# Row sums of a small-attention group: from GpSimd additions in SBUF to identity matmuls on TensorE in PSUM

## Chip, cores and metric

One NeuronCore of a Trainium2 chip runs the whole kernel in a single launch. The metric is the device time of one execution in microseconds. The kernel before took 4007.05 us, the median of three runs (4005.77 to 4012.08).

## What is computed

The input x is [8, 512, 256] in fp32, and four residual layers follow each other, each on a layer norm of x:

```python
x = x + attn_a(layernorm(x))   # 16 heads of C = 64; see below
x = x + ffn(layernorm(x))      # silu gate, two gelu layers of 1024, back to 256
x = x + attn_b(layernorm(x))   # ordinary causal attention over 512 tokens, 16 heads of 16
x = x + ffn(layernorm(x))      # the same weights again
```

Attention A is the odd one. It attends not over tokens but over the 64 channels of one head of one token:

```python
Q, K, V = (x @ W + b).reshape(b, s, 16, 64)       # Q scaled by 1/8
scores[q, k] = Q[q] * K[k]     for k <= q          # an outer product per head and token
w = softmax(scores, axis=k)
attn[q] = sum_k w[q, k] * V[k]
x_out = attn.reshape(b, s, 1024) @ Wo + bo
```

So nothing of the scores is a matmul: each token and head has a 64x64 triangle of products, exponentials and weighted sums, with tokens on the partitions.

## The kernel before

**Groups and units.** Attention A goes through 8 batches b, 4 groups of heads g (4 heads, GW = 256 channels) and 4 token tiles i of 128: 128 groups. In each group the triangle is cut into a diagonal and squares: squares of 32 rows and columns, then of 16, 8, 4, 2 and 1. They make four units u: unit 0 is the squares of 32 of heads 0 and 1, unit 1 the squares of 16 of all four heads, unit 2 the squares of 32 of heads 2 and 3, unit 3 all smaller squares. Units 0 to 2 have 2048 scores per token and use a work tile w of 4096 elements, which holds the exponentials in one half and the exponentials times V in the other; unit 3 has 1920 and uses the tile ws.

**One unit's way.** `scores` (the multiplication at L784) writes Q times K: for units 0 and 2 on GpSimd, for units 1 and 3 on VectorE, which reads Q from the PSUM tile qv. `exps` (L798) takes the exponential on ScalarE. `weigh` (L808) multiplies by V on VectorE, again with qv in PSUM as one operand. `halve` (L814), for units 0 to 2, is a DMA issued from GpSimd's queue that adds one half of the columns of w onto the other, 1 MB each. `fold` (L819), for units 0 and 2, halves once more on GpSimd. `gather` (L845) reduces what is left along the columns to row sums red, on VectorE. The diagonal's exponential and its product with V are in acc, [128, 2, 256]: plane 0 for the denominators, plane 1 for the numerators.

**Ending a group.** `add_rows` (L852) adds the row sums of each size to the rows of acc to which they belong, on GpSimd, seven additions per group; for squares of 2 and 1 `small_squares` takes them from ws itself, after an addition of pairs (L835). `invert` (L856) is VectorE's reciprocal of plane 0, `divide` (L860) GpSimd's product. `turn_group` (L868) transposes plane 1 on TensorE, ScalarE copies it to att (L719), `project_out` (L876 and L472) multiplies by Wo and adds x, and `new_x` (L887) copies the new x back.

**Buffers.** The PSUM tile `bank` is one bank of two halves of 256 columns. `half_bank` hands the halves out in turn, to the layer norm's transpose, the projection of K (`project`, L741), `turn_group` and `project_out`. qv, the projection of Q and V (L746), has two buffers. Tile w has three buffers for units 0 and 2; unit 1 has a tile of its own, w16, with one; ws has one.

**What sets the order.** The order of TensorE, VectorE, ScalarE and GpSimd is the order of the program text (`manual_schedule`). Each engine works off its own queue in order. Step n of `AttentionA.step` begins unit n and does the later work of earlier units: `self.at(n - 2)` is the unit that began two steps ago. So a group is four steps, and "n - 5 with u == NU - 1" means five steps after the group's last unit began. Each step has three parts, parted by `yield`. After each part the main loop takes as many pieces from the second stream (FFN, attention B, FFN of the batch that A has finished) as a planned cost allows: `total = 309.5` units per batch, spread evenly over its 64 steps, beginning after the first 64 steps and eleven more. That stream is `after_a`; its ffn matmuls are L1052, L1120 and L1146. In the first batch attention A is alone, after the last one the stream is alone.

The scheduling of the group's end before, cut from the step:

```python
b, i, g, u = self.at(n - 5)
if u == NU - 1:
    self.invert(b, i, g)
...
yield
...
for args in self.sums:
    self.add_rows(*args)
...
```

Of the kernel before, what the change touches and what calls it, by code (L numbers as in the profile page):

```python
# [284 lines left out]
def fast_path(ctx: ExitStack, tc: tile.TileContext, k, t, flag):  # L285
# [196 lines left out]

    bank = ps_a.tile([P, 2, GW], F32, name="bank")
    halves = [0]

    def half_bank():
        halves[0] ^= 1
        return bank[:, halves[0], :]
# [115 lines left out]
    class AttentionA:  # L604
# [3 lines left out]
        def __init__(self):  # L608
            self.x = {0: x_first}
            self.rn, self.live = {}, {}  # L610
            self.w = {(0, 0): fitted[0]}
            self.wo = {}
            self.load_wo(0, 0)
            self.ready, self.sums = set(), []
            self.todo = [
                (b, i, g, u) for b in range(NB) for g in range(NG) for i in range(NT) for u in range(NU)
            ]
            self.steps = len(self.todo) + 11
# [19 lines left out]
        def step(self, n):  # L638

            weighed = self.at(n - 2)  # L640
            if weighed[0] is not None:
                self.weigh(*weighed)
            unit = self.at(n)
            on_pool = unit[3] in (0, 2)
            if on_pool:
                half = self.scores(*unit)
                next(half)
            if weighed[0] is not None:
                self.halve(*weighed)
            if on_pool:  # L650
# [11 lines left out]
            if u == NU - 1:  # L662
                self.invert(b, i, g)
            b, i, g, u = self.at(n - 4)
            if u == 1:
                self.gather(b, i, g, u)
            b, i, g, u = self.at(n + 7)
            if u == 0 and g == 0:
                nc.scalar.copy(self.live[b, i], self.live.pop("ps_ln"))
            if self.at(n - 1)[0] is not None:  # L670
                self.exps(*self.at(n - 1))
            yield
            if unit[0] is not None and not on_pool:
                for _ in self.scores(*unit):
                    pass
            for args in self.sums:
                self.add_rows(*args)
            self.sums = []
            b, i, g, u = self.at(n - 5)
            if u == NU - 1:  # L680
                self.divide(b, i, g)
            b, i, g, u = self.at(n - 2)
            if u == NU - 1:
                self.small_squares(b, i, g)

            b, i, g, u = self.at(n - 4)
            if u == 0:
                self.fold(b, i, g, u)
# [3 lines left out]
            b, i, g, u = self.at(n - 9)  # L692
            if u == NU - 1:
                self.new_x(b, i, g)
            b, i, g, u = self.at(n + 2)
            if u == 0:
                self.keep_qk(b, i, g)
            b, i, g, u = self.at(n - 7)
            if u == NU - 1:
                self.turn_group(b, i, g)  # L700
            b, i, g, u = self.at(n - 8)
# [9 lines left out]
            b, i, g, u = self.at(n - 5)  # L711
            if u == 0:
                self.gather(b, i, g, u)
# [3 lines left out]
            b, i, g, u = self.at(n - 7)  # L717
# [3 lines left out]
            if u == 0 and g == 0:  # L721
                self.live[b, i] = lnp.tile([P, DC, P], F32, tag="xnt_a", name=f"xnta_{b}_{i}", bufs=NT)
                self.live["ps_ln"] = turned_over(self.live.pop("xn"), half_bank().rearrange("p (c s) -> p c s", c=DC))
# [11 lines left out]
        def project(self, b, i, g):  # L735
# [3 lines left out]
            pk = half_bank()  # L739
# [25 lines left out]
        def scores(self, b, i, g, n_u):  # L765
# [6 lines left out]

            if n_u in (0, 2):
                w = wt.tile([P, 4096], F32, tag="w", name=f"w_{b}_{i}_{g}_{n_u}", bufs=3)
            elif n_u == 1:
                w = wt.tile([P, 4096], F32, tag="w16", name=f"w16_{b}_{i}_{g}")
# [3 lines left out]
            eng, q = (nc.gpsimd, kt[:, 1]) if n_u in (0, 2) else (nc.vector, qv[:, 0])  # L780
# [47 lines left out]
        def small_squares(self, b, i, g):  # L828

            w = self.live[b, i, g, NU - 1]  # L830
            for n, off, nsq, cols in squares(units[NU - 1]):
                if n <= 2:
                    both = self.columns_of(w, n, off, nsq)
                    if n == 2:
                        nc.gpsimd.tensor_tensor(both[..., :1], both[..., :1], both[..., 1:], ALU.add)  # L835
                    self.add_rows(b, i, g, n, cols, both[..., 0])

        def gather(self, b, i, g, n_u):


            w = self.live.pop((b, i, g, n_u))
            for n, off, nsq, cols in squares(units[n_u]):
                if n > 2:
                    red = ap_.tile([P, 2, nsq * n], F32, tag=f"red{nsq * n}", name=f"red_{b}_{i}_{g}_{n_u}_{n}", bufs=2 + (n < 32))
                    nc.vector.tensor_reduce(red, self.columns_of(w, n, off, nsq), AX.X, ALU.add)  # L845
                    self.sums.append((b, i, g, n, cols, red))

        def add_rows(self, b, i, g, n, cols, part):

            acc = self.live[b, i, g][2]  # L850
            rows = acc[:, :, cols].rearrange("p a (x t) -> p a x t", t=2 * n)[..., n:]
            nc.gpsimd.tensor_tensor(rows, rows, part.rearrange("p a (x i) -> p a x i", i=n), ALU.add)  # L852

        def invert(self, b, i, g):
            acc = self.live[b, i, g][2]
            nc.vector.reciprocal(acc[:, 0, :], acc[:, 0, :])  # L856

        def divide(self, b, i, g):
            acc = self.live[b, i, g][2]
            nc.gpsimd.tensor_tensor(acc[:, 1, :], acc[:, 1, :], acc[:, 0, :], ALU.mult)  # L860

        def turn_group(self, b, i, g):
# [3 lines left out]
            pt = half_bank().rearrange("p (c s) -> p c s", c=nch)  # L866
# [577 lines left out]
```

## Time and profile before

| What | Value |
|---|---|
| median of three runs | 4007.05 us |
| the profiled execution | 4009.55 us |
| its span | 4007.6 us |
| PE busy | 2958.0 us, 74% |
| DVE busy | 3376.7 us, 84% |
| ACT busy | 2337.2 us, 58% |
| POOL busy | 3098.1 us, 77% |
| DMA, mean rate | 167 GB/s |

The engines are PE (TensorE matmuls), PEld (its weight loads, which overlap the matmuls), DVE (VectorE), ACT (ScalarE), POOL (GpSimd) and SP (SyncE, which here issues DMAs). A line such as L784 is a line of the kernel before. A group of instructions is shown as line, engine, operation, output <- inputs by the program's names, shapes, count, then busy us in total, mean ns of one, and the engine's idle time just ahead of them with what ended it. A window row has its start and end, its length, the busy us of PE, PEld, DVE, ACT and POOL (with the number of instructions), the granted TensorE clock as a share of full speed, the mean busy share of the 16 DMA engines and their GB/s. In the records each fp32 matmul of the program appears twice.

### The profile page before, as it was taken

The page shows a single profiled execution, that of the slowest core. Times are in us where ns is not written, and L with a number is a line of the kernel's source. Part 1 is how long each engine was busy: PE and PEld are TensorE (multiplying, and loading weights), DVE is VectorE, ACT ScalarE, POOL GpSimd, SP SyncE. Part 2 cuts the span into 40 slices and gives each one's busy share as a digit, 9 for nine tenths or more (in the row PEclk, how much of TensorE's full clock was granted, in tenths as well). Part 3 has the DMA queues.
Part 4 walks back from the last instruction along what each step waited for, and adds up shares of the span by engine and source line. Part 5 has one row for each costly group of instructions (what it writes and reads, how often), then busy time and mean ns, then how long its engine had stood idle before and what let it go on. Part 6 is the DMA issues. An engine that isn't in the chain of part 4 may idle for free.

```text
span 4007.6 us, 37678 instructions
## 1 busy us (share of the span) xinstructions
PE 2958.0 (74%) x12328; PEld 2012.2 (50%) x12328; DVE 3376.7 (84%) x3777; ACT 2337.2 (58%) x3145; POOL 3098.1 (77%) x3051
## 2 busy tenths in 40 slices
PE   1543478777876888768787788768787778768988
PEld 0311145355653656346553566346653556436847
DVE  4899988998889888998989988998889988897115
ACT  2433465666755766666755767567656667555342
POOL 6688888887888887887888888888888878886211
PEclk7555689888987989889897889879898899879999
DMA  8566777668776777668776688668877687767304
GB/s 240 114 141 145 146 182 182 147 161 199 199 162 126 195 188 196 150 147 210 174 192 139 168 198 214 147 131 198 195 181 151 154 199 205 155 133 210 126 29 167
DMA packets 118653, 671.07 MB, mean 167 GB/s; under 512 B 12704, under 2 KB 31915, under 8 KB 43824
## 3 DMA queue, kind: packets, MB, share of 16 engines
q0 software_dynamic: 78336, 570.46, 62.9%
q1 hardware_dynamic: 40112, 98.11, 6.8%
q8 instruction: 100, 1.64, 0.2%
q14 instruction: 105, 0.86, 0.1%
HBM read 255.90 MB, written 9.96 MB: 66 GB/s over the span
## 4 chain that ended last, share of the span: by engine, by line
DVE 38%; PE 16%; POOL 14%; DMA 12%; issue 8%; ACT 8%; POOLq 0%; DVEq 0%; ACTq 0%
DVE red L845 15%; DMA w<-w 12%; DVE w L808 10%; PE ph L1120 5%; ACT w L798 3%; POOL w L819 3%; DVE ws L808 3%; POOL w L784 3%; PE pqkb L1167 3%; DVE ws L784 3%; POOL acc L852 3%; DVE w L784 2%; POOL w L814 2%; DVE acc L856 2%; POOL h L1036 2%
## 5 line engine op out<-in xcount | busy, mean ns | idle before, releaser
L798 ACT ACTIVATE w<-w 128x2048 f32<-128x2048 f32 x384 | 734.2, 1913 | 653.8 <-POOL w L784 440.8
L1120 PE MATMUL ph<-h,hidden 128*128 128x512 f32 x4096 | 1047.9, 412 | 77.4 <-POOL h L1036 45.5
L784 POOL TENSOR_TENSOR w<-k 128x1024 f32<-128x1024 f32 x512 | 1076.2, 2102 | 9.6 <-ACT k L762 9.0
L1120 PEld LDWEIGHTS ph<-h,hidden 128*128 128x128 f32 x4096 | 795.3, 196 | 282.1 <-POOL h L1036 55.9
L808 DVE TENSOR_TENSOR w<-w,qv 128x1024 f32<-128x1024 f32 x768 | 899.8, 1213 | 22.4 <-ACT w L798 22.3
L845 DVE TENSOR_REDUCE red<-w 128x128 f32<-128x1024 f32 (+1 forms) x384 | 601.8, 1567 | 171.6 <-DMA w<-w 94.6
L819 POOL TENSOR_TENSOR w<-w 128x1024 f32<-128x1024 f32 x256 | 643.1, 2512 | 72.5 <-DMA w<-w 71.9
L814 POOL DMA_DIRECT2D w<-w x384 | 337.1, 878 | 339.7 <-issue 134.8
L852 POOL TENSOR_TENSOR acc<-acc,red 128x256 f32<-128x256 f32 (+1 forms) x640 | 471.0, 736 | 152.3 <-DVE red L845 124.5
L845 DVE TENSOR_REDUCE red<-ws 128x256 f32<-128x2048 f32 (+1 forms) x256 | 435.5, 1743 | 0.0
L746 PE MATMUL qv<-wqv,xnta 128*128 128x512 f32 x512 | 299.3, 715 | 89.9 <-DVE ws L808 82.4
L808 DVE TENSOR_TENSOR ws<-ws,qv 128x1024 f32<-128x1024 f32 (+3 forms) x512 | 294.7, 638 | 49.4 <-ACT ws L798 49.4
L1052 PE MATMUL pw<-xnt,gate 128*128 128x512 f32 (+2 forms) x1152 | 298.8, 419 | 24.9 <-ACT silu L1028 18.0
L784 DVE TENSOR_TENSOR w<-qv,k 128x1024 f32<-128x1024 f32 x256 | 301.3, 1219 | 3.6
L784 DVE TENSOR_TENSOR ws<-qv,k 128x1024 f32<-128x1024 f32 (+3 forms) x512 | 299.8, 648 | 0.0
L868 PE MATMUL bank<-ident,acc 128*128 128x128 f32 x256 | 64.3, 341 | 287.5 <-ACT k L761 287.1
L798 ACT ACTIVATE ws<-ws 128x1920 f32<-128x1920 f32 x128 | 231.5, 1809 | 75.3 <-DVE ws L784 74.7
L1052 PEld LDWEIGHTS pw<-xnt,gate 128*128 128x128 f32 x1152 | 227.6, 213 | 82.1 <-ACT silu L1028 22.3
L1229 ACT ACTIVATE eb<-psb 128x256 f32<-128x256 f32 (+3 forms) x512 | 182.2, 443 | 146.6 <-PE psb L1226 146.3
L1146 PE MATMUL pof<-w,h 128*128 128x256 f32 x1024 | 247.9, 396 | 19.4 <-ACT h L1085 19.4
L1085 ACT ACTIVATE h<-ph,s_sb 128x512 fp32r<-128x512 f32 (+1 forms) x256 | 171.1, 688 | 145.9 <-PE ph L1120 144.6
L856 DVE RECIPROCAL acc<-acc 128x256 f32<-128x256 f32 x128 | 223.2, 1744 | 12.3 <-POOL acc L852 12.3
(143 smaller groups left out, 4723.5 us busy)
## 6 DMA issues: line engine op xcount, KB each, us to landing
w<-w POOLq DMA_DIRECT2D x384, 1024.0 KB, 7.7
hidden<-in_h POOLq DMA_DIRECT2D x128, 1024.0 KB, 7.9
gate<-in_w12p POOLq DMA_DIRECT2D x32, 1024.0 KB, 9.0
w<-w_d SPq DMA_DIRECT2D x16, 1024.0 KB, 12.0
wqv<-wqv_d SPq DMA_DIRECT2D x31, 512.0 KB
wo<-in_wo SPq DMA_DIRECT2D x32, 256.0 KB, 7.4
wbqk<-wbqk_d SPq DMA_DIRECT2D x8, 1024.0 KB
w<-in_h SPq DMA_DIRECT2D x8, 1024.0 KB, 7.0
```

The source lines that it names most:

```text
L746: nc.tensor.matmul(qv.rearrange("p j f -> p (j f)"), xnt[:, c, :], wqv[:, c, :], start=(c == 0), stop=(c == DC - 1),)
L784: eng.tensor_tensor(e, rows(q).to_broadcast(shape), columns(kt[:, 0]).to_broadcast(shape), ALU.mult)
L798: nc.scalar.activation(e, e, AF.Exp, scale=C**-0.5)
L808: nc.vector.tensor_tensor(ev, e, columns(qv[:, 1]).to_broadcast(list(e.shape)), ALU.mult)
L814: nc.gpsimd.dma_start(w[:, :2048], w[:, 2048:], accum_op=ALU.add)
L819: nc.gpsimd.tensor_tensor(w[:, :1024], w[:, :1024], w[:, 1024:2048], ALU.add)
L845: nc.vector.tensor_reduce(red, self.columns_of(w, n, off, nsq), AX.X, ALU.add)
L852: nc.gpsimd.tensor_tensor(rows, rows, part.rearrange("p a (x i) -> p a x i", i=n), ALU.add)
L856: nc.vector.reciprocal(acc[:, 0, :], acc[:, 0, :])
L1052: nc.tensor.matmul(pj[:, toks], w[:, m % 4, j, c, :], xs[:, p, c, toks], start=(p == 0 and c == 0), stop=(p == 1 and c == DC - 1),)
L1120: nc.tensor.matmul(pss[j], w[:, j, c, :], h_in(p, c), start=(p == 0 and c == 0), stop=(p == 1 and c == MC - 1),)
L1146: nc.tensor.matmul(po, h(0, c)[:, i * P : (i + 1) * P], w3[:, c, :], start=(c == 0), stop=False)
```

## The change

Five things change together.

1. `add_up` replaces `add_rows` and `small_squares`. On TensorE, the identity as the stationary operand, a first matmul copies acc (512 columns) into `bank`, and eight more add the row sums to the strided rows of it to which they belong: the sums of the squares of 32 (two, 128 columns each), of 16, 8 and 4 (256 each) from red, those of 2 as two matmuls of 256 columns (one for each column of the square) and those of 1 (256) straight from ws. Both halves of `bank` are taken while this lasts.
2. `divide` takes reciprocal and product on VectorE, with `bank` as an operand of both; the result is written to acc as before.
3. The scores of unit 1 (the squares of 16) go to GpSimd: two pieces of 1024 elements per partition.
4. Units 0, 1 and 2 share one rotation of four w tiles; w16 is gone. The red tiles have one buffer for each unit and size.
5. The halves of `bank` are fixed: half 0 for layer norm and K, half 1 for turn and output. The steps are placed anew (below); unit 0's halve is put ahead of both score pieces of unit 2; the lag at which the second stream starts falls from eleven steps to ten; and in `after_a` the first batch's four tiles of layer norm are set off with a flush and 0.8 units of cost each.

The steps after the group's last unit, before and after (part in brackets): row sums 1 to 4 by size -> `add_up` 4 [2]; reciprocal 5 [1] and product 5 [2] -> both 5 [1]; turn 7 [2] -> 6 [1]; output product 8 [2] -> 7 [2]; new x 9 [2] -> 8 [1].

The core of the diff:

```diff
             unit = self.at(n)
-            on_pool = unit[3] in (0, 2)
-            if on_pool:
+            large = unit[3] in (0, 1, 2)
+            if weighed[0] is not None and weighed[3] == 0:
+                self.halve(*weighed)
+            if large:
                 half = self.scores(*unit)
                 next(half)
-            if weighed[0] is not None:
+            if weighed[0] is not None and weighed[3] > 0:
                 self.halve(*weighed)
...
+            b, i, g, u = self.at(n - 4)
+            if u in (0, 1):
+                self.gather(b, i, g, u)
...
             b, i, g, u = self.at(n - 5)
             if u == NU - 1:
-                self.invert(b, i, g)
+                self.divide(b, i, g)
...
+            b, i, g, u = self.at(n - 6)
+            if u == NU - 1:
+                self.turn_group(b, i, g)
             yield
...
+            b, i, g, u = self.at(n - 4)
             if u == NU - 1:
+                self.add_up(b, i, g)
...
             b, i, g, u = self.at(n - 3)
             if u == NU - 1:
                 self.gather(b, i, g, u)
+            if u == 0:
+                self.fold(b, i, g, u)
+            if unit[0] is not None and not large:
+                for _ in self.scores(*unit):
+                    pass
...
-            if n_u in (0, 2):
-                w = wt.tile([P, 4096], F32, tag="w", name=f"w_{b}_{i}_{g}_{n_u}", bufs=3)
-            elif n_u == 1:
-                w = wt.tile([P, 4096], F32, tag="w16", name=f"w16_{b}_{i}_{g}")
+            if n_u < NU - 1:
+                w = wt.tile([P, 4096], F32, tag="w", name=f"w_{b}_{i}_{g}_{n_u}", bufs=4)
             else:
                 w = wt.tile([P, 2 * SMALL], F32, tag="ws", name=f"ws_{b}_{i}_{g}")
-            eng, q = (nc.gpsimd, kt[:, 1]) if n_u in (0, 2) else (nc.vector, qv[:, 0])
+            eng, q = (nc.gpsimd, kt[:, 1]) if n_u < NU - 1 else (nc.vector, qv[:, 0])
...
+        def add_up(self, b, i, g):
             acc = self.live[b, i, g][2]
+            parts = self.live.pop(("parts", b, i, g))
+            nc.tensor.matmul(bank, ident, acc, start=True, stop=False)
+            for j, (n, cols, part) in enumerate(parts):
+                rows = bank[:, :, cols].rearrange("p a (x t) -> p a x t", t=2 * n)[..., n:]
+                part = part.rearrange("p a (x i) -> p a x i", i=n)
+                nc.tensor.matmul(rows, ident, part, start=False, stop=j == len(parts) - 1)
 
         def divide(self, b, i, g):
             acc = self.live[b, i, g][2]
-            nc.gpsimd.tensor_tensor(acc[:, 1, :], acc[:, 1, :], acc[:, 0, :], ALU.mult)
+            nc.vector.reciprocal(acc[:, 0, :], bank[:, 0])
+            nc.vector.tensor_tensor(acc[:, 1, :], bank[:, 1], acc[:, 0, :], ALU.mult)
...
         for i in range(NT):
             head(0, i)
+            flush()
+            yield 0.8
...
-                while 3 * spent * each < total * (3 * (n - each - 11) + part + 1):
+                while 3 * spent * each < total * (3 * (n - each - 10) + part + 1):
```

## The prediction, made before the result

> **What bounds the kernel now.** I read the page's engine totals first, then its chain of what ended last.
>
> ```profile
> span 4007.6 us, 37678 instructions
> PE 2958.0 (74%) x12328; PEld 2012.2 (50%) x12328; DVE 3376.7 (84%) x3777; ACT 2337.2 (58%) x3145; POOL 3098.1 (77%) x3051
> DVE 38%; PE 16%; POOL 14%; DMA 12%; issue 8%; ACT 8%; POOLq 0%; DVEq 0%; ACTq 0%
> ```
>
> VectorE is fullest, GpSimd second, TensorE close behind. The totals mix stages, so next the windows by stage (columns: window, length, then busy us of PE, PEld, DVE, ACT, POOL, then granted clock, DMA share, GB/s).
>
> ```profile
> 86.00:473.00 387.00, 160.76 (x347) 84.94 (x347) 357.53 (x373) 145.71 (x147) 312.05 (x274) 0.56 0.66 140
> 473.00:1394.00 921.00, 700.54 (x2920) 472.42 (x2920) 832.03 (x937) 579.31 (x777) 769.02 (x757) 0.86 0.73 171
> 1394.00:1634.00 240.00, 195.36 (x754) 143.53 (x754) 205.89 (x229) 153.34 (x187) 195.53 (x198) 0.90 0.78 190
> 1634.00:1855.00 221.00, 164.87 (x774) 102.96 (x774) 208.55 (x240) 145.29 (x214) 187.95 (x181) 0.85 0.70 159
> 1855.00:3588.00 1733.00, 1351.03 (x5772) 922.75 (x5772) 1559.53 (x1744) 1114.91 (x1499) 1442.20 (x1411) 0.87 0.74 175
> ```
>
> The 128 reciprocals (L856), one per group, are the clock of attention A. In the first stage (A alone) they follow each other by 23.7 us and VectorE never rests. From 473 us on, with the feed-forward stream (FFN and attention B) beside A, they average 28.70 us (475.6 to 3574.8 us, 108 steps); there VectorE is busy 832+206+209+1560 = 2806 of 3115 us, 25.9 per group, and TensorE 2412 us, 22.2 per group. So A alone is bound by VectorE; the mixed stage has 2.8 us of VectorE idle per group and 6.5 us of TensorE idle. After 3588 us A runs out and the last stream is alone; the change doesn't touch that tail. The prices come from groups by shape, window 500 to 3500 us (104 groups), then the lone-A stage.
>
> ```profile
> L784 POOL TENSOR_TENSOR w<-k 128x1024 f32<-128x1024 f32 x416 | 875.5, 2105 | 0.6
> L784 DVE TENSOR_TENSOR w<-qv,k 128x1024 f32<-128x1024 f32 x208 | 244.8, 1219 | 2.8
> L852 POOL TENSOR_TENSOR acc<-acc,red 128x256 f32<-128x256 f32 x311 | 236.4, 760 | 114.9 <-DVE red L845 92.2 <-PE pyt L1268 5.7
> L852 POOL TENSOR_TENSOR acc<-acc,ws 128x256 f32<-128x256 f32 x208 | 166.0, 798 | 16.3
> L852 POOL TENSOR_TENSOR acc<-acc,red 128x128 f32<-128x128 f32 x208 | 145.4, 699 | 0.0
> L860 POOL TENSOR_TENSOR acc<-acc 128x256 f32<-128x256 f32 x104 | 106.3, 1022 | 0.0
> L835 POOL TENSOR_TENSOR ws<-ws 128x256 f32<-128x256 f32 x104 | 72.8, 700 | 0.0
> L856 DVE RECIPROCAL acc<-acc 128x256 f32<-128x256 f32 x104 | 181.4, 1744 | 11.1 <-POOL acc L852 11.1
> ...
> L746 PE MATMUL qv<-wqv,xnta 128*128 128x512 f32 x48 | 45.0, 1094 | 23.0 <-DVE ws L808 17.4 <-issue 5.7
> ```
>
> The timeline near 2015 us gives what runs of matmuls really occupy (start, length).
>
> ```profile
> 2014.85 1.02 PE L741 MATMUL bank<-wk,xnta 128*128 128x256 f32 x4
> 2015.71 1.88 PE L746 MATMUL qv<-wqv,xnta 128*128 128x512 f32 x4
> ...
> 2024.38 0.41 PE L868 MATMUL bank<-ident,acc 128*128 128x128 f32 x2 [1.33 <-ACT k L761]
> ```
>
> **What the skill says.** "FP8 and Floating Point Precision", TensorE Precision Notes: true fp32 takes four passes. The trace shows two records per fp32 matmul, and L746's four records (two matmuls of 512 columns) have weight loads 0.43 us apart, so 1.72 us, 1.68 ns a column. "TensorE: Matmul & The Clock Gate", What's actually happening: an idle array runs at half clock. The trace agrees: lone-A clock 0.56, L746 at 1094 ns. "GPSIMD Engine Reference", Engine selection: GpSimd has no way to PSUM, so with sums there the quotient must go elsewhere; no row shows GpSimd on PSUM.
>
> **The change, part by part, per group.**
> GpSimd loses seven additions (L852: 3x0.76 + 2x0.80 + 2x0.70 = 5.3), the product (1.02) and the pair sum (0.70): -7.0 us. It gains two score pieces, 2x2.1 = +4.2. Net -2.8. GpSimd isn't on the loop below, so this gains nothing by itself; it gives back some of the DMA slack lost below.
> VectorE loses two pieces, 2x1.22 = -2.4. It gains the quotient's product; the nearest PSUM-reading row of that size (L771) takes 0.42. The reciprocal now reads PSUM: 1.74 taken; at least that, since no reason makes it shorter, at most 0.1 more. Net -2.0: 25.9 becomes 23.9.
> TensorE gains nine identity matmuls over 512 + 128 + 256 + 128 + 256 + 256 + 2x256 + 256 columns (acc, the squares of 32, 16, 32, 8, 4, 2 as two, 1): 2304 columns x 1.68 = 3.9, plus weight loads on the short ones; I take 4.2. Matmuls with strided reads and writes have no row: 3.9 if the stride is free, since columns can't cost less than contiguous ones, and 7.8 at half clock (4.2 x 1094/592, the full-clock length of L746). Total 22.2 + 4.2 = 26.4, now above VectorE.
> Steps: the first fold, turn, output product and new x come one step earlier. What each issues goes along: the wo load on SP's queue moves up with the output product, with a group's length before its data are used; keep_qk moves up within its step on ACT, which is busy 19 of 28.7 us. Cost nil under that cover; without it, one copy, 0.4 us per group. The stream and so the tail begin one of four steps sooner: -28.7/4 = -7 us once. The stagger at the stream's head (four flushes) lies beside A; uncovered it would be a few us once.
> Halves: the first w's DMA had 20.7 us of VectorE work between weighing and its reduction (two reductions of ws and one of w 4.6, three weighings 7.0, L784 for ws and w16 4.7, L845 of w16 2.3, L771 and L856 2.2), now 11.6 (4.6, two weighings 4.6, ws scores 2.4); less the 2.5 us fold, 9.1 stay. The squares of 16 get 10.8 for 9.1, the third w 8.6 for 10.5. DMA landing is 7.8 us in median, 16.7 at most, in the mixed stage. Zero in lone A (8.0 at most), up to a few us where weights load. With the rotation of four, scores on GpSimd wait for a reduction at least one step old: nil.
>
> **The new wait** is what decides. ws has one buffer and the row sums read it on TensorE. So VectorE's small scores must wait until the last identity matmul ends, and behind them on VectorE stand the third weighing, the first reduction and the quotient; TensorE's turn waits for the quotient, and the whole stream stands behind the turn. That is a closed loop, whose length no slack shortens:
> on VectorE, small scores to quotient: 2.26 + 2.26 + 1.13 + 0.34 + 1.66 + 0.35 = 8.0 (scores, third weighing, first reduction, L771, reciprocal, product, as the timeline's starts follow each other), plus 5/12 of the stream's 2.2 us (L1031, L1091, L524, L983, L525, L1262 over 104 groups) = 8.9;
> on TensorE, turn 0.4, projection 0.86 + 1.72 = 2.6, output 1.3, seven of twelve parts of the stream (22.2 less A's own 4.3 = 17.9, so 10.4), row sums 4.2: 18.9.
> Sum 27.8; a hand-over is short (the att copy starts 0.03 us after the turn's end at 2024.8). TensorE's idle today is 6.5 per group, 2.2 of it at the turn (226.4 us over 104 groups), which the loop replaces; of the other 4.3, seven twelfths, 2.5, can lie in the loop. Bounds: 0 to 2.5; I take 1.4: less than the bound, since TensorE no longer runs ahead of ACT, but late DMAs are in it. Result 29.2: +0.5 over 28.7, x112 groups = +56 us.
> Lone A: 8.0, then VectorE's 11.5 from the quotient to the last reduction (weighings 2.2 and 2.6, reductions 2.2, 1.1 and 3.3), then the four matmuls that need it or come after, eight passes: 4.2 us at half clock (L876 there: 52 records in 26.9 us), 1.7 at full. So 23.7 or 21.8 (VectorE's own 23.7 - 1.9) against 23.7: bounds 0 and -1.9. I take -0.4, the clock being low in this stage: x15 = -6 us.
> Sum: 56 - 6 - 7 = +43. The profiled execution took 4009.55 us, so 4052.6; the median of the runs is 2.5 less: 4050.
>
> **The rivals.**
> A: faster. The half-clock share of TensorE's time vanishes as it gets denser, and the idle inside the loop is near 0. Then dense groups (half, PE 195 of 240 us) stay as they are, light ones gain 0.6: -34; lone A gains all 1.9: -28; -7. 3940. For it: clock 0.85 to 0.90 now, and both fullest engines get lighter. Against: the loop. It decides where the mean reciprocal distance falls under 28.82 (28.70 + 13/112).
> B: worse. The idle in the loop is the full 2.5 and DMAs past 9.1 us stop the first reduction inside it: +1.4 x 112 - 13 = +144: 4150. For it: in the dense stretch (1394 to 1634 us) VectorE already waited 12.8 us for the w DMA and 11.6 for the fold behind it, in 8 groups.
> C: gain and loss cancel: the mixed stage at +0.1, near 4005.
>
> **Chances.** Forecast 0.47, A 0.30, B 0.10, C 0.13. Under 0.2% this kernel's measurement tells nothing, so C splits 0.04 faster, 0.09 same. Faster 0.34, same 0.09, slower 0.57. Range 3920 to 4170: it takes in A's and B's centres with about 0.1 left out below and 0.06 above; the forecast alone is 4000 to 4100.
>
> **What would show it.** Right: VectorE idle before the small scores with TensorE as releaser, some us per group; reciprocals about 29 us apart; PE near 26 us per group; lone A near 23.3. Wrong: that wait absent or under 1 us with reciprocals below 28.5 apart (the loop isn't the bound), row sums far from 4.2 us, or VectorE's added idle ending on DMA w instead.

## The result and the profile after

The changed kernel takes 4330.07 us (median of four runs) against 4009.57 us for the kernel before on the same chip: 1.0801 times as long, 95% interval 1.0783 to 1.0820. The forecast was 4050 us with a range up to 4170: the direction came out as forecast, the size is outside the range. The profiled execution has a span of 4328.0 us, 320.4 more than before.

In the listings of the changed kernel the lines are numbered anew: scores are L769, exps L783, weigh L793, halve L799, fold L804, the reductions L821, the copy of acc into the bank L830, the other row sums L834, reciprocal and product L838 and L839, the turn L847, the output product L855 and L472, the new x L866, the projections of K and of Q and V L729 and L734, the copy of K out of the bank L749, the turn of the stream's layer norm L544.

First the page's span, engine totals and chain of the changed kernel.

```profile
span 4328.0 us, 41431 instructions
...
PE 3405.4 (79%) x14632; PEld 2385.9 (55%) x14632; DVE 3154.8 (73%) x3649; ACT 2360.3 (55%) x3161; POOL 2851.6 (66%) x2155
...
PE 43%; DVE 26%; ACT 12%; POOL 9%; issue 7%; DMA 3%; SPq 0%; ACTq 0%; POOLq 0%; DVEq 0%
```

VectorE and GpSimd did get lighter (by 222 and 246 us), and TensorE took 447 us more. No engine is above 79%, yet the kernel is 8% longer. The chain of what ended last has changed hands: TensorE 43% (16% before), VectorE 26% (38%). Next the windows of the changed kernel for A alone and for the mixed stage, then that of the kernel before for the same mixed stretch.

```profile
86.00:473.00 387.00, 209.26 (x640) 127.47 (x639) 348.29 (x380) 157.89 (x158) 304.52 (x181) 0.74 0.71 150
```

```profile
600.00:3600.00 3000.00, 2454.88 (x10722) 1733.04 (x10721) 2272.00 (x2653) 1770.18 (x2361) 2077.90 (x1565) 0.91 0.67 158
```

```profile
600.00:3600.00 3000.00, 2332.86 (x9957) 1588.78 (x9958) 2704.22 (x3034) 1921.17 (x2591) 2495.06 (x2452) 0.87 0.74 173
```

The second row is the changed kernel, the third the one before. In the mixed stage every engine but TensorE does less in the same 3000 us, and the DMAs move 158 instead of 173 GB/s: the whole kernel waits for something. A group's reciprocals are 31.84 us apart there (from the 17th to the third last), 28.81 before; in A alone (2nd to 15th) 22.30 against 23.88. The account of the 320.4 us: up to the 17th reciprocal the changed kernel is 13.4 us ahead (485.9 against 499.3 us, although its first reciprocal comes 13.7 us later, at 100.0 instead of 86.3); from there to the last reciprocal it loses 332.6 us (3521.7 against 3189.1); behind that the tail is as long as before (320.4 and 319.2). So all of the loss lies in the mixed stage.

The waits of the changed kernel say for what, in 600 to 3700 us (columns: engine, what it wanted and its line, the releaser; us in total, times, longest).

```profile
DVE ws L769 <- PE bank L834: 521.6, 90, 11.0
POOL w L799 <- DVE w L793: 518.9, 154, 9.6
ACT ws L783 <- DVE ws L769: 221.9, 44, 8.6
...
PE bank L847 <- DVE acc L839: 136.5, 46, 6.1
```

The first line is the wait that the prediction named: VectorE stands before the small scores until the last identity matmul has read ws, 5.3 us for each of the 98 groups whose small scores start in this window. The second and third are what stands behind it: GpSimd's halve and ScalarE's exponentials wait for VectorE in turn. In A alone the same wait is 1.3 us once, in 200 to 500 us.

One round of the loop, in the timeline of TensorE and then of VectorE (start, length):

```profile
2010.74 0.59 PE L472 MATMUL pof<-x,ident 128*128 128x256 f32 x2
2011.17 0.38 PE L847 MATMUL bank<-ident,acc 128*128 128x128 f32 x2
...
2024.15 0.69 PE L544 MATMUL ps_ln<-ident,xn 128*128 128x128 f32 x2 [4.21 <-ACT xn L534]
...
2027.67 1.92 PE L830 MATMUL bank<-acc,ident 128*128 128x512 f32 x2
2029.38 3.62 PE L834 MATMUL bank<-red,ident 128*128 128x128 f32 x10
2032.79 1.73 PE L834 MATMUL bank<-ws,ident 128*128 128x256 f32 x6
2034.17 5.84 PE L1031 MATMUL pw<-xnt,gate 128*128 128x512 f32 x24
```

```profile
2007.49 0.42 DVE L839 TENSOR_TENSOR acc<-bank,acc 128x256 f32<-128x256 f32 x1
...
2018.18 3.40 DVE L821 TENSOR_REDUCE red<-ws 128x256 f32<-128x2048 f32 x2
...
2034.56 2.35 DVE L769 TENSOR_TENSOR ws<-qv,k 128x1024 f32<-128x1024 f32 x4 [4.31 <-PE bank L834]
...
2042.33 0.42 DVE L839 TENSOR_TENSOR acc<-bank,acc 128x256 f32<-128x256 f32 x1
```

VectorE ends the quotient at 2007.91. TensorE turns it only at 2011.17, behind stream matmuls that stood earlier in its queue. Then come A's projection, stream, output product, and a stretch in which TensorE waits for the layer norm of a stream tile (4.21 us before L544). The row sums begin at 2027.67 although the last reduction they read had ended at 2021.6. They read ws last, so VectorE starts the next small scores at 2034.56, and the next quotient ends at 2042.75: one round of 34.8 us.

### The profile page after: what moved, and what is told of

Its sections match the earlier page's. It is cut to its first block, busy times and chain, and to the rows that moved or that the text cites. A ratio compares the mean times of both kernels' runs of the same rounds, so it can differ in the third digit from the quotient of the medians.

```text
span 4328.0 us, 41431 instructions
## 1 busy us (share of the span) xinstructions
PE 3405.4 (79%) x14632; PEld 2385.9 (55%) x14632; DVE 3154.8 (73%) x3649; ACT 2360.3 (55%) x3161; POOL 2851.6 (66%) x2155
## 4 chain that ended last, share of the span: by engine, by line
PE 43%; DVE 26%; ACT 12%; POOL 9%; issue 7%; DMA 3%; SPq 0%; ACTq 0%; POOLq 0%; DVEq 0%
PE ph L1099 12%; PE bank L834 8%; DVE w L793 7%; DVE red L821 7%; POOL w L769 4%; DVE acc L838 3%; PE qv L734 3%; DVE ws L769 3%; ACT w L783 3%; PE bank L830 3%; PE pqkb L1146 3%; PE pw L1031 2%; DMA w<-w 2%; PE bank L855 2%; PE pyb L1213 2%
## 5 line engine op out<-in xcount | busy, mean ns | idle before, releaser
L769 POOL TENSOR_TENSOR w<-k 128x1024 f32<-128x1024 f32 x768 | 1601.4, 2240 | 9.3 <-ACT k L750 9.3
L1099 PE MATMUL ph<-h,hidden 128*128 128x512 f32 x4096 | 1034.4, 408 | 5.8 <-POOL h L1015 4.5
L799 POOL DMA_DIRECT2D w<-w x384 | 344.9, 898 | 986.5 <-DVE w L793 607.0
L793 DVE TENSOR_TENSOR w<-w,qv 128x1024 f32<-128x1024 f32 x768 | 898.7, 1211 | 5.3 <-ACT w L783 5.3
L1099 PEld LDWEIGHTS ph<-h,hidden 128*128 128x128 f32 x4096 | 783.2, 193 | 194.6 <-issue 19.7
L783 ACT ACTIVATE w<-w 128x2048 f32<-128x2048 f32 x384 | 735.7, 1916 | 199.3 <-POOL w L769 198.2
L769 DVE TENSOR_TENSOR ws<-qv,k 128x1024 f32<-128x1024 f32 (+3 forms) x512 | 300.5, 649 | 588.4 <-PE bank L834 588.4
L804 POOL TENSOR_TENSOR w<-w 128x1024 f32<-128x1024 f32 x256 | 634.1, 2477 | 143.6 <-DMA w<-w 141.1
L821 DVE TENSOR_REDUCE red<-w 128x128 f32<-128x1024 f32 (+1 forms) x384 | 600.8, 1565 | 39.9 <-POOL w L804 39.5
L821 DVE TENSOR_REDUCE red<-ws 128x256 f32<-128x2048 f32 (+1 forms) x256 | 435.3, 1741 | 0.0
L783 ACT ACTIVATE ws<-ws 128x1920 f32<-128x1920 f32 x128 | 231.7, 1810 | 295.4 <-DVE ws L769 288.6
L793 DVE TENSOR_TENSOR ws<-ws,qv 128x1024 f32<-128x1024 f32 (+3 forms) x512 | 298.8, 645 | 14.3 <-ACT ws L783 14.3
L834 PE MATMUL bank<-red,ident 128*128 128x256 f32 (+1 forms) x1280 | 293.3, 377 | 20.1 <-DVE red L821 19.9
L834 PEld LDWEIGHTS bank<-red,ident 128*128 128x128 f32 x1280 | 233.9, 218 | 131.7 <-issue 79.5
L734 PE MATMUL qv<-wqv,xnta 128*128 128x512 f32 x512 | 290.3, 696 | 8.2 <-DVE ws L793 8.1
L847 PE MATMUL bank<-ident,acc 128*128 128x128 f32 x256 | 66.9, 352 | 275.1 <-DVE acc L839 267.7
L855 PE MATMUL bank<-wo,att 128*128 128x256 f32 x512 | 151.0, 420 | 117.3 <-ACT k L749 117.2
L830 PE MATMUL bank<-acc,ident 128*128 128x512 f32 x256 | 165.6, 734 | 85.2 <-ACT x L866 79.5
```

The costliest lines, as they stand in the source:

```text
L734: nc.tensor.matmul(qv.rearrange("p j f -> p (j f)"), xnt[:, c, :], wqv[:, c, :], start=(c == 0), stop=(c == DC - 1),)
L769: eng.tensor_tensor(e, rows(q).to_broadcast(shape), columns(kt[:, 0]).to_broadcast(shape), ALU.mult)
L783: nc.scalar.activation(e, e, AF.Exp, scale=C**-0.5)
L793: nc.vector.tensor_tensor(ev, e, columns(qv[:, 1]).to_broadcast(list(e.shape)), ALU.mult)
L799: nc.gpsimd.dma_start(w[:, :2048], w[:, 2048:], accum_op=ALU.add)
L804: nc.gpsimd.tensor_tensor(w[:, :1024], w[:, :1024], w[:, 1024:2048], ALU.add)
```

## The experiments

Each distance below is that between reciprocals, as above.

| Kernel | us | ratio to before (95%) | A alone | mixed |
|---|---|---|---|---|
| before | 4009.6 | 1 | 23.88 | 28.81 |
| changed | 4330.1 | 1.0801 (1.0783-1.0820) | 22.30 | 31.84 |
| e1, ws read first | 4162.6 | 1.0374 (1.0350-1.0397) | 22.2 | 30.33 |
| e2, acc copied twice | 4441.7 | 1.1073 (1.1052-1.1094) | 22.5 | 32.86 |
| e3, 16s to VectorE | 4432.2 | 1.1049 (1.1027-1.1071) | 25.7 | 32.44 |
| e4, 2s and 1s to GpSimd | 4129.7 | 1.0295 (1.0274-1.0316) | 23.75 | 29.86 |
| e5, 2s and 1s in own tile | 4085.8 | 1.0173 (1.0151-1.0196) | 22.2 | 29.59 |
| e6, e4 with 16s on VectorE | 4154.2 | 1.0342 (1.0319-1.0365) | 24.3 | 30.05 |
| e7, sums a part earlier | 4268.3 | 1.0639 (1.0621-1.0657) | 22.2 | 31.26 |
| e8, e7 with ws first | 4159.2 | 1.0368 (1.0350-1.0386) | 22.4 | 30.26 |
| e9, one-pass sums | 4189.1 | 1.0440 (1.0418-1.0461) | 22.8 | 30.58 |
| e10, e5 and e9 | 4039.1 | 1.0068 (1.0052-1.0085) | 22.25 | 29.17 |
| e11, e5 with 16s on VectorE | 4202.5 | 1.0484 (1.0465-1.0502) | 24.4 | 30.43 |
| e12, change in A alone only | 4037.1 | 1.0061 (1.0044-1.0078) | 24.5 | 28.87 |
| e13, before, short slack | 4047.0 | 1.0088 (1.0072-1.0105) | 24.5 | 29.04 |
| e14, before, more matmuls | 4064.3 | 1.0128 (1.0111-1.0145) | 23.9 | 29.29 |
| e15, e12 with the new order | 4001.7 | 0.9981 (0.9971-0.9990) | 22.5 | 28.85 |
| e16, e13 and e14 | 4122.5 | 1.0280 (1.0266-1.0294) | 24.6 | 29.69 |

### Is the loop through ws the bound? (e1, e2)

e1 lets the matmuls that read ws come first after the copy of acc. No work is added or taken away; only ws comes free earlier.

```diff
-            parts = self.live.pop(("parts", b, i, g))
+            parts = sorted(self.live.pop(("parts", b, i, g)), key=lambda p: p[0])
```

> Only the order of the row sums' matmuls is changed, so that those that read ws come directly after the copy of acc and five others (1024 columns, some 1.7 us) follow. Loop theory (the small scores on VectorE wait for the last matmul that reads ws, and TensorE's turn waits for the quotient behind them): VectorE starts 1.7 us earlier in each of the 112 mixed groups, -190 us, near 4140. Rival 1 (TensorE is simply full, the wait on ws only shows that): nothing changes, 4330 within 0.5%. Rival 2 (VectorE, GpSimd or DMA sets the time): nothing changes either.

It measured 4162.6 us, 1.5 us per mixed group less than the changed kernel, and nothing in A alone. The wait fell with it (e1, 600 to 3700 us):

```profile
DVE ws L769 <- PE bank L834: 349.7, 93, 9.7
```

A mere reordering on an engine that is 79% busy won half of the loss. What follows is that the time between the start of the row sums and the release of ws is in the bound.

e2 is the opposite test: the copy of acc is done twice, so that TensorE holds ws longer by one matmul of 512 columns.

```diff
             nc.tensor.matmul(bank, ident, acc, start=True, stop=False)
+            nc.tensor.matmul(bank, ident, acc, start=True, stop=True)
```

(the added one stands ahead of the old one.)

> The copy of acc into the bank is issued twice, which adds 512 columns in fp32 to TensorE (0.9 us) in each group and nothing elsewhere. Loop theory and rival 1 (TensorE full): +0.9 us in each of 112 mixed groups, +100 us, near 4430. Rival 2 (VectorE, GpSimd or DMA sets the time): within 0.5% of 4330.

4441.7 us, as the loop expects: +1.02 us per mixed group for a matmul of 0.9 us at full clock. In a kernel whose bound has slack at this place, part of it would have vanished. A TensorE that is simply full would show the same, so e2 alone doesn't tell the two apart; e1, where TensorE's work is the same, does.

### Taking load from the loop or from other engines (e3, e4, e6, e7, e8)

e3 gives the scores of the squares of 16 back to VectorE, inside the changed kernel.

```diff
-            eng, q = (nc.gpsimd, kt[:, 1]) if n_u < NU - 1 else (nc.vector, qv[:, 0])
+            eng, q = (nc.gpsimd, kt[:, 1]) if n_u in (0, 2) else (nc.vector, qv[:, 0])
```

> The scores of the squares of 16 go back to VectorE, all else stays as changed. Loop theory: their 2.4 us lie between the quotient and the last reduction, where VectorE waits 5 us per group for TensorE later on, so the mixed stage stays as it is; attention A alone, bound by VectorE, gets back about 2 us per group, +30 us: near 4360. Rival 2a (VectorE's load sets the time): +2.3 us in each of 128 groups, near 4620. Rival 2b (GpSimd's load sets it): 100 us or more faster.

4432.2 us is between the two. In the mixed stage 2.4 us more on VectorE cost 0.6 us, so VectorE's load isn't the bound, but not free either; in A alone they cost 3.4, more than the 2.4 themselves.

e4 takes the reads of ws off TensorE: the squares of 2 and 1 are added to acc on GpSimd as in the kernel before (`small_squares`, two steps after their scores), ahead of the row sums. That opens the loop and shortens the row sums by three matmuls.

```diff
+            b, i, g, u = self.at(n - 2)
+            if u == NU - 1:
+                self.small_squares(b, i, g)
...
-                else:
-                    parts += [(n, cols, both[..., j]) for j in range(n)]
```

> The squares of 2 and 1 are added to acc on GpSimd again (three instructions, 2.3 us there), so TensorE reads ws no more and the small scores have nothing to wait for; TensorE has three matmuls less (1.3 us), and the first red has two buffers. Loop theory: the loop is open, the group is bound by TensorE's own 25.3 us and its remaining waits, some 28 us instead of 31.8: -420 us, near 3920. Rival 1 (TensorE full): only the 1.3 us go, -145 us, near 4185. Rival 2: within 1% of 4330.

The loop is gone and 200 us with it, but 4129.7 us is far from the 3920 that I expected. A new chain had taken its place (e4: the page's chain, then two waits in 600 to 3600 us):

```profile
POOL 31%; PE 24%; DVE 21%; issue 12%; ACT 11%; DMA 1%; POOLq 0%; SPq 0%; ACTq 0%; DVEq 0%
```

```profile
DVE red L824 <- POOL w L807: 180.8, 81, 6.5
...
POOL w L807 <- DMA w<-w: 117.3, 44, 5.4
```

VectorE's first reduction waits for GpSimd's fold, and the fold for the transfer ahead of it. I took GpSimd's load for the cause, and e6 relieves it by moving the squares of 16 to VectorE as in e3.

> As the last kernel with the squares of 2 and 1 on GpSimd, but the scores of the squares of 16 back on VectorE: GpSimd 4.2 us lighter per group, VectorE 2.3 heavier. Second theory (GpSimd's row binds once the loop is open): the mixed stage gains about 1 us per group and attention A alone loses about 0.5, 4020 to 4050 against 4130. Rival (VectorE's load binds there): +2 us per group, near 4350.

4154.2 us, slower than e4, and the fold waits even longer for the transfer (e6, 600 to 3600 us):

```profile
POOL w L807 <- DMA w<-w: 180.5, 83, 7.5
```

GpSimd's load as the only cause fell. The test isn't a clean one, since e6 loads VectorE with 2.4 us more.

e7 puts `add_up` one part of a step earlier, so that fewer stream matmuls stand before the row sums; e8 adds the order of e1.

```diff
+            b, i, g, u = self.at(n - 4)
+            if u == NU - 1:
+                self.add_up(b, i, g)
             yield
...
-            b, i, g, u = self.at(n - 4)
-            if u == NU - 1:
-                self.add_up(b, i, g)
```

> The row sums' matmuls come one part of a step earlier in TensorE's queue, so that one twelfth of the stream (1.5 us) moves out of the stretch from turn to row sums into the one that lies beside VectorE's small scores and quotient. Nothing else changes. Loop theory: -1.5 us x 112 = -165, near 4165. Rival 1 (TensorE full): no change, since TensorE's work is the same.

> Both: one part earlier, and the matmuls that read ws first. Loop theory: the two savings add up as long as the loop binds, -165 and -167: near 4000. If another bound takes over (TensorE's 26.6 us with its waits, or GpSimd's row), the second saving is cut: 4060 to 4130.

e7 won 62 us of the 165 expected: the stretch from turn to row sums shrank from 17.30 to 16.22 us, but the row sums with the hand-over to the next scores grew from 4.91 to 5.28 us. e8 ended where e1 did, so the two gains don't add. TensorE's wait for the bank ahead of the row sums (L830, for the copy of the new x) is 62.1 us in the changed kernel, 85.7 in e7 and 88.4 in e8 (600 to 3600 us): with fewer matmuls in front, TensorE comes to the bank before it is free.

### The loop opened with TensorE's work kept (e5), and a lighter TensorE (e9, e10), and the load of VectorE again (e11)

e5 keeps all identity matmuls. The squares of 2 and 1 get a tile of their own, wl, with two buffers, and ws holds the rest. VectorE's next scores then write another wl than the one TensorE reads. To make room, att and a layer norm buffer have one buffer instead of two, and the exponential of the small unit comes in two instructions.

```diff
-                w = wt.tile([P, 2 * SMALL], F32, tag="ws", name=f"ws_{b}_{i}_{g}")
+                w = (
+                    wt.tile([P, 2 * MAIN], F32, tag="ws", name=f"ws_{b}_{i}_{g}"),
+                    wt.tile([P, 2 * (SMALL - MAIN)], F32, tag="wl", name=f"wl_{b}_{i}_{g}", bufs=2),
+                )
```

> The squares of 2 and 1 get a tile of their own with two buffers (room for it: one buffer less for att and for the layer norm's xn of A and B; their exponential becomes a second, short ACT instruction); no other work moves. The small scores no longer wait for TensorE; the first reduction, 4.5 us later on VectorE, still does (its red has one buffer). Loop theory alone: the loop gets up to 4.5 us shorter and TensorE's own 26.6 us plus waits bind, 27.5 to 28.5 us per group instead of 31.8: 3900 to 3960. Second theory, after the last run (with the loop open, GpSimd's row of halve, DMA and fold binds next): near 29.5 us per group, 4080. Rival 1 (TensorE is full anyway): above 4250.

4085.8 us: 2.2 of the 3.0 us per mixed group are gone, with no work taken from any engine. The wait of VectorE's small scores for the row sums is gone from the list of waits (e5, 600 to 3700 us; chain ahead of it):

```profile
PE 39%; DVE 23%; POOL 14%; ACT 11%; issue 8%; DMA 5%; SPq 0%; POOLq 0%; ACTq 0%; DVEq 0%
```

```profile
POOL w L810 <- DMA w<-w: 198.1, 113, 6.7
...
DVE red L828 <- POOL w L810: 113.7, 55, 6.5
PE bank L862 <- ACT k L750: 113.1, 63, 3.8
```

So the loop is 2.2 us of the loss. The other 0.8 us have another cause or several: TensorE carries 39% of the chain, and the pair fold after transfer, reduction after fold has come up as in e4.

In e9 the changed kernel's acc and its sums of the squares of 4 and more are written in the one-pass fp32 format, so that each identity matmul which reads them has one record in the trace instead of two (at 2042.74 us in e9 the copy of acc takes 0.23 us until the next matmul starts); those of ws stay as they were. e10 does the same in e5, with one buffer less for the stream's layer norm.

```diff
-            nc.tensor.matmul(bank, ident, acc, start=True, stop=False)
+            nc.tensor.matmul(bank, ident_r, acc, start=True, stop=False)
...
-                nc.tensor.matmul(rows, ident, part, start=False, stop=j == len(parts) - 1)
+                nc.tensor.matmul(rows, ident_r if n > 2 else ident, part, start=False, stop=j == len(parts) - 1)
```

> Changed kernel with acc and the reductions of more than 2 columns written as fp32r, and their six identity matmuls (1536 columns) in fp32r, one pass instead of four[...]. The matmuls of the squares of 2 and 1 stay fp32. By the rates of this case (1.68 ns a column in fp32, 227 ns for 512 columns in fp32r) TensorE has 1.9 us less per group, all in the loop. Loop theory: 31.8 becomes 29.9, -215 us, near 4115. Rival 2 (VectorE, GpSimd or DMA): unchanged, 4330.

> The same fp32r sums in the kernel whose squares of 2 and 1 have a tile with two buffers (loop opened, 29.6 us per group, 4086 us; one buffer less for the stream's xn). If what binds after the loop is TensorE's own work with its waits: 1.9 us less per group, 27.7, near 3875, faster than the kernel before. If GpSimd's row of halve, DMA and fold binds there: within 1% of 4086.

e9 won 141 us, two thirds of what I expected, at a granted clock of 0.869 instead of 0.894. e10 won 47 us over e5, 0.4 us per mixed group: of the 0.8 us about half goes with TensorE's work. It didn't fall to the 3875 us that a pure TensorE bound would have given.

e11 puts the squares of 16 back on VectorE in e5.

> Loop opened as before, and the scores of the squares of 16 back on VectorE: GpSimd 4.2 us lighter, VectorE 2.3 heavier, TensorE as it was. If TensorE binds the mixed stage after the loop: that stage stays at 29.6 us per group, and attention A alone gets 2 us per group slower, +30: near 4115. If GpSimd's row binds: about 1 us per group less, near 4000. If VectorE binds: +2.3 us per group, near 4350.

4202.5 us, between the theories again, and the fold now waits far longer for transfers (e11, 600 to 3600 us):

```profile
POOL w L810 <- DMA w<-w: 547.3, 115, 10.6
```

The transfers themselves land in 7.7 us in median, against 7.8 in e5, so they aren't slower. That they start later, because the scores moved to VectorE delay weighing, is the likely reading; no run tests it alone.

### The rest, in the kernel before (e13, e14, e16)

e5 leaves two suspects, and both can be put into the kernel before one at a time. e13 shortens the time that the first large tile's transfer has: its halve comes ahead of the scores, and its fold and its reduction come earlier, as in the changed kernel (the expectation below calls the fold later, which its edit is not: it moves from the second part of one step to the third part of the step before). No instruction is added. e14 computes the projection of Q and V three times: four more matmuls of 512 columns per group, 2048 columns against the 2304 of the row sums, without a wait for other data; only qv itself is ready later.

```diff
+            if weighed[0] is not None and weighed[3] == 0:
+                self.halve(*weighed)
...
-            b, i, g, u = self.at(n - 4)
-            if u == 0:
-                self.fold(b, i, g, u)
```

```diff
-            for c in range(DC):
+            for c in range(3 * DC):
```

> The kernel before, with only the fold of the first large tile one step later, its reduction some steps earlier and its transfer started ahead of the next scores, as in the changed kernel: no operation is added. If the shorter time for that transfer (my sum: 18.2 to 9.1 us) is what keeps the opened loop 0.8 us per mixed group above the kernel before: +0.4 to +0.8 us x 112 groups, 4055 to 4100. If it isn't: within 0.5% of 4010.

> The kernel before, with the projection of Q and V computed three times instead of once: per group four more matmuls of 512 columns, 2048 columns or 3.4 to 4.5 us of TensorE, about the row sums' load, with no new wait for another engine's data. If TensorE's added work alone keeps the opened loop 0.8 us per mixed group above the kernel before: +0.4 to +0.8 us x 112 groups, 4055 to 4100. If TensorE's 6.5 idle us per group hide it: 4010.

> The two edits of e13 (shorter time for the first transfer) and e14 (the matmuls of Q and V three times) together in the kernel before. Alone they measured +35 and +52 us. If they add up, and so stand for what is left in the opened loop (e5_split, 1.0173): +87, near 4097, ratio 1.02. If they share one slack and hide each other: 4065.

Each alone costs: 4047.0 us (+0.9%), just under the span given for it, and 4064.3 us (+1.3%). From the 17th to the last reciprocal e13 loses 25 us against before, e14 53, both together (e16) 97, and e5 88. So 2048 needless columns of fp32 in an engine with 6.5 us of idle time per group are not free: about 0.5 us per group (the later qv is in this figure). And the shorter slack is about 0.2 us, and 0.4 where TensorE is loaded (29.69 in e16 against 29.29 in e14). In e13 the waits show the pair that e4 and e5 had shown (600 to 3600 us; in the kernel before the second line had 70.0 us):

```profile
ACT w L796 <- POOL w L782: 404.9, 117, 7.6
...
DVE red L843 <- POOL w L817: 126.6, 71, 7.7
```

The two suspects give 97 us where e5 shows 88. That fits in size; it is not a proof that e5 holds nothing else, since its VectorE and GpSimd are lighter than those of the kernel before.

### The gain of A alone by itself (e12, e15)

e12 is the kernel before, with the change in the first 16 groups only, and the row sums in a free bank of the stream's.

```diff
+            on_pool = n_u in (0, 2) or (n_u == 1 and b == 0)
+            eng, q = (nc.gpsimd, kt[:, 1]) if on_pool else (nc.vector, qv[:, 0])
...
+            total = self.live["total"] = ps_f.tile([P, 2, GW], F32, tag="pf", name=f"total_{i}_{g}")
+            nc.tensor.matmul(total, ident, acc, start=True, stop=False)
```

> The kernel before, with the change in the lone-A stage alone (the first 16 groups): scores of the squares of 16 on GpSimd, row sums by identity matmuls into a free bank of the stream's, those that read the small tile first and ahead of the next small scores, quotient by VectorE. If the changed kernel's gain in lone A (23.9 to 22.3 us per group) is the lighter VectorE and nothing in the mixed stage is touched: 22.2 to 22.6 us there, some 15 x 1.5 = 23 us less, near 3985, faster than both kernels. If that gain came of the other order or the rotation of four: no gain, 4010. If the sums at half clock stand in the way: above 4010.

A miss: 24.5 us per group, slower than before, although VectorE's busy time in 86 to 473 us fell from 357.5 to 318.3 us. The waits show why (e12, 86 to 473 us):

```profile
ACT w L802 <- POOL w L788: 170.8, 42, 9.1
...
POOL w L788 <- DVE red L852: 42.2, 14, 25.6
...
DVE red L852 <- POOL w L823: 33.8, 14, 2.6
```

With one tile for the squares of 16, GpSimd stands for VectorE's reduction before it can write the next scores, its fold stands behind that, and VectorE then waits 2.4 us per group for the fold. The relief of VectorE turned into a circle of waits between the two. e15 takes over the rotation of four tiles and the order of the changed kernel for these groups, and leaves the very first group as before.

```diff
+                tag = "w16" if self.large % 4 == 2 else "w"
+                self.large += 1
```

> As the kernel of e12 (the change in the first 16 groups alone), with these groups' steps, rotation of four tiles and place of the scores of 16 taken over from the changed kernel too, and the very first group scored as before. In e12 GpSimd waited for the one tile of 16s and VectorE behind it for the fold (24.5 us per group). If the changed kernel's gain in lone A needs the rotation of four and the order: 22.3 us per group here, up to 15 x 1.6 = 24 us less than before, 3986 to 4000. If the hand-over into the mixed stage costs it again, as in e12: 4010 or more.

22.5 us per group, as in the changed kernel, and 4001.7 us: 0.9981 times before, interval 0.9971 to 0.9990. It is faster than both kernels, by a hair. Its first reciprocal comes 8.2 us later than before, but at the 17th it is 13.7 us ahead (485.7 against 499.4 us); of these the mixed stage takes back 4.6 us and the tail 2.8, so that some 6 us remain in the profiled executions and 8 in the medians. Since e15 takes over the rotation and the order together, it doesn't tell which of the two gave the gain.

## Why the prediction was wrong in size

**The loop: right.** It named the wait, its releaser, the edge ws, and what stands behind it. e1 and e5 show that the loop costs 2.2 of the 3.0 us per mixed group, and e2 agrees. It isn't closed in every round: of the 109 rounds from the 17th to the third last reciprocal, VectorE's small scores wait for the row sums in 100, and TensorE starts the turn within 0.1 us of the quotient's end in 60. In the other 49 TensorE comes to the turn later, so that its own queue from the row sums to the turn is the longer way there.

**The sum of the loop: the step that failed.** It gave 29.2 us; the timeline gives 31.84. Term by term, as means over these 109 rounds of the changed kernel:

| Term | forecast | measured |
|---|---|---|
| small scores to end of quotient, VectorE | 8.9 | 8.34 |
| hand-over, quotient to turn | 0.03 | 1.30 |
| turn to row sums, TensorE busy | 14.7 | 14.06 |
| turn to row sums, TensorE idle | 1.4 | 3.24 |
| row sums, and hand-over to the next scores | 4.2 | 4.91 |
| sum | 29.2 | 31.84 |

Two terms of waiting carry the miss; the two busy terms above them were high by 1.2 us together and hide a part of it. The hand-over of 0.03 us was read from a place where the waiting engine had nothing else in its queue (ScalarE's copy after the turn). Here the waiting engine is TensorE, and the turn stands in its queue behind stream matmuls, as at 2007.91 to 2011.17 us above: the median is 0.06 us, and the mean comes from the 49 rounds in which TensorE comes late. And the idle of 1.4 was argued down from a bound of 2.5; it is above the bound. The waits of TensorE name what fills it (changed kernel, 600 to 3600 us, 94 groups):

```profile
PE ps_ln L544 <- ACT xn L534: 93.8, 36, 8.9
...
PE bank L855 <- ACT k L749: 87.6, 55, 3.0
...
PE bank L830 <- ACT x L866: 62.1, 25, 4.4
...
PE ps_ln L544 <- ACT xn L538: 37.2, 16, 3.6
```

The stream's layer norm (first and last line) is 1.4 us per group, by itself as much as the forecast for all idle time. The other two, 1.6 us per group, are waits for the one bank, and the sum of the loop had no term for them. The row sums take both halves of it and so wait for the copy of the new x. The output product waits for the copy of K, though K lies in half 0 and the product goes to half 1, and its own input had long been there: at 1204.08 us it starts 0.06 us after K's copy ends, 3.6 us after att was copied. What makes the program set this wait isn't shown here. In the kernel before the same copy held up the turn (the 2.2 us of idle time which the prediction took as replaced by the loop); in the changed kernel part of that wait has moved to the output product and lies inside the circle. Idle that was harmless when TensorE had 6.5 us per group to spare became length of a loop without slack.

**Row sums: a little low.** 4.2 had been taken at nearly full clock, from the price of 1.68 ns a column. The median round takes 4.24 us with the hand-over; the mean is higher because of rounds like the one shown above, where TensorE had stood idle and the granted clock was 0.57 (2022 to 2034 us): there the copy of acc has 1.71 us before the next matmul starts, 3.3 ns a column. That is in line with what the prediction quotes of the Trainium skill's "TensorE: Matmul & The Clock Gate", What's actually happening, on an idle array's clock. Strided rows have no price of their own that would show: the median stays within 0.4 us of the 3.9 for contiguous columns.

**TensorE's load.** 26.4 us per group were forecast, 26.1 are measured (2454.9 of 3000 us, 31.84 us a group).

**A alone: right in sign, low in size.** 23.3 was forecast, 22.30 came: TensorE's clock rose with its load (0.56 to 0.74), so the half-clock bound didn't hold. But the later start takes 13.7 us back, so that 13.4 us are left at the 17th group, where 6 were forecast. The 7 us for a stream that begins one step earlier should have shortened the tail behind the last reciprocal; it is 320.4 us against 319.2, so they don't show.

**Claims of no cost.** The rotation of four: no such wait leads. The halved slack of the first tile had no term of its own in the forecast, which left late transfers inside the idle of 1.4, and was half of rival B: by itself it costs 0.2 us (e13), and with more load on TensorE more (e16). It is hidden in the changed kernel, whose loop is longer; VectorE's reduction waits 14.7 us for the fold there (600 to 3600 us). The reciprocal takes 1745 ns in mean from PSUM, against 1744 before, as taken.

**The rivals.** B pointed the right way with the idle at its bound of 2.5 and gave 4150; the second half of its story, the transfer, isn't what made the size. B's sum also falls short of its own terms: 27.8 + 2.5 is 1.6 us over 28.7, not 1.4, which gives some 4170. A's light engines did appear, and gained only where no loop is. The two waiting terms exceed the forecast's by 3.1 us together (1.27 + 1.84), where B, near the top of the range, had allowed for 1.4 us over the kernel before in all.

**What stays open.** What is left in e10 (0.36 us per mixed group) isn't told apart further. The waits for the bank were read from the trace and no run takes them away: a second bank for the row sums in the mixed stage wasn't tried, nor were moving halves instead of the fixed ones. So their 1.6 us per group are a measured part of the round, but what the kernel would gain without them isn't known.

## What to carry to other kernels

When work that reads a single buffered tile goes to another engine, follow the edge from the last read back to the next write, and add up the whole circle: busy time, and every place where an engine of the circle has other work queued ahead or waits for a third engine. List the waits of the whole circle by name, for every shared buffer that it crosses, rather than taking a share of today's idle time: here even the upper bound taken that way was too low. And when the kernel gets longer while every engine but the one that took on work is less busy than before, such a circle is a good guess: look for the one wait that stands in front, and test it by reordering the reads before redesigning anything.

## What the runs showed that I had not expected

- Matmuls that wait for nothing new still cost: in the kernel before, 2048 more fp32 columns per group beside 6.5 us of idle time made it 1.3% longer (e14), although the granted clock rose from 0.845 to 0.895.
- A matmul into one half of the bank waited for a copy out of the other half (L855 for L749, 87.6 us in 94 groups), although its own input was there.
- One-pass sums gave two thirds of the time they should: the granted clock over the run was 0.869 instead of 0.894 with the lighter TensorE (e9).
- VectorE lighter by 11% in A alone made A alone slower (e12: 357.5 to 318.3 us busy, 23.9 to 24.5 us a group), until tile rotation and order came along (e15).
